# First block of a two-block transformer: a two-list scheduler replaced by one written program, PSUM pairs replaced by a ring of eight banks

## The chip, the cores and the metric

The kernel runs on one core of a Trainium2 chip. TensorE (PE) multiplies matrices and transposes; its results go to PSUM, which here is used as eight banks of 128 partitions by 512 float32 numbers. ScalarE (ACT), VectorE (DVE) and GpSimd (POOL) do the elementwise work, and only they empty PSUM banks. SyncE (SP) starts most DMA transfers. The engines run side by side, each through its own list of instructions in order, and wait for each other by semaphores. The metric is the device time of one execution in microseconds (us), the median of several.

## The reference

x is 8 x 512 x 256 in float32 (8 batches of 512 rows), with a condition per batch and 64 context tokens per batch. Block 1, per batch:

```python
mod = silu(c) @ adaln_w.T + adaln_b          # nine vectors of 256: shift, scale, gate of each part
h = modulate(ln(x), shift_sa, scale_sa)
q, k, v = ln(heads(h, 16)), ln(heads(h, 16)), heads(h, 16)   # times and plus learned rows
x = x + gate_sa * unheads(softmax(q k^T / 4) v)
h = modulate(ln(x), shift_ca, scale_ca)      # cross attention, 16 heads of 16, 64 keys
x = x + gate_ca * (unheads(softmax(q kb^T / 4) vb) @ ca_out_w.T + ca_out_b)
h = modulate(ln(x), shift_ff, scale_ff)      # feed forward, 1024 wide
x = x + gate_ff * ((silu(h @ w1.T) * (h @ w3.T)) @ w2.T)
```

Block 2 has self attention with 16 heads of 64 and rotary embeddings, cross attention, and a feed forward with gelu. Everything is float32.

## The kernel before

**Block 1's tiling.** A batch's 16 heads are handled as four groups g of four heads, and the 512 keys as four key tiles kt of 128. One unit (`block`, L593) is one group with one key tile. Its four score matmuls (L603) contract over 16 rows each and stand in four row strips of the array, so they run together as a quad; they write two PSUM tiles of two banks (`bank_s`), each emptied by one exp on ACT of 128x1024 (L606) into a p tile. Its four value matmuls (L612) make 32 columns each in four column strips, also together, and add up over the key tiles in `bank_o`; v has a column of ones, so the softmax denominator comes along. Before a group, `queries_keys` (L580) transposes the normalized heads into a bank, ACT makes q of it (L589), DVE k (L590). After a group, `group_end` (L617) copies ps_O to oT on ACT (L619), and `group_back` (L622) transposes oT into a bank; DVE takes the denominator, inverts, multiplies and checks, POOL applies the gate and adds to x.

The per-head layernorm is made a batch ahead: `norm` (L518), then for each half c of the heads `head_centre` (DVE, L558 to L560), `head_square` (ACT, L564), `head_var` (DVE) and `head_scale` (POOL: a power of 5.4 us, a product of 1.06 us).

`batch2` (L683) is the cross attention of a batch, one cycle later: `prepare` (layernorm), `turn` (eight transposes to hT), `queries`, two units `block(c)` with scores of 32 rows and values, the latter with a copy of the denominators on ACT (den, L733, one buffer), two DMAs out and one back (L736 to L738), `inverse`, `scaled`, and `project_out`. `batch3` (L769) is the feed forward, two cycles later: eight `up(f)` (four full matmuls of 512 columns, a tanh on ACT, L797, two products on DVE), and `down(t)` for four row tiles (L801).

**Order.** `run_blocks` (L51) writes the program out. A batch is a cycle of 18 units: 16 of self attention, and two of the cross attention of the batch before at places 11 and 13. Other steps are registered with `at(i, fn)` and `then(i, fn)` (L498, L501) at a unit's number. In the first cycle each unit stands alone: its scores, the values of the unit before, the other steps. Later the units go in twos: scores(i), steps registered at i-2 and i-1, scores(i+1), values(i-1), values(i), and then the steps of the list `behind`. At the start, three `awake` matmuls stand on either side of the first group's preparation to keep PE busy.

**PSUM.** S: two tiles of two banks. O: one bank. D: one. X: two. `bank_x()` (L119) takes D and X in turn for everything that is not a score or a value product of self attention. Every engine that empties a bank so decides when PE may write to it again.

**Block 2** opens its own PSUM pools (`pair`, name ps_P, and others) with `other_banks` (L993); its first matmul stands at 831.19 us in the timeline. `last_out` (L1135) takes two pairs for the last self-attention output.

Of the kernel before, what the change touches and what calls it, by code (L numbers as in the profile page):

```python
# [10 lines left out]
F32 = mybir.dt.float32  # L11
# [7 lines left out]
P = 128  # L19
# [25 lines left out]
class Block:  # L45


    def __init__(self, scores, values):
        self.scores, self.values = scores, values


def run_blocks(blocks, beside, behind, alone):

    def scores(i):
        for fn in blocks[i].scores if i < len(blocks) else []:
            fn()

    def values(i):
        for fn in blocks[i].values if 0 <= i < len(blocks) else []:
            fn()

    def others(i):
        for fn in beside.get(i, []):
            fn()

    others(-1)
    for i in range(alone):  # L70
        scores(i)
        values(i - 1)
        others(i)
    scores(alone)
    values(alone - 1)
    for i in range(alone + 1, max(len(blocks) + 2, *(k + 3 for k in (*beside, *behind))), 2):
        scores(i)
        if i > alone + 1:
            others(i - 2)
        others(i - 1)  # L80
        scores(i + 1)
        values(i - 1)
        values(i)
        for fn in (*behind.get(i - 2, []), *behind.get(i - 1, [])):
            fn()


def fast_path(ctx: ExitStack, tc: tile.TileContext, a: dict, out: bass.AP):
# [28 lines left out]

    def bank_x():
        turns[0] += 1  # L119
        n = turns[0] % (2 + len(extra))  # L120
        if n < len(extra):
            return extra[n]()
        return psum.tile([P, 512], F32, tag="X", name="ps_X", bufs=2)

    extra.append(bank_d)
# [137 lines left out]
    mod = sp.tile([P, 768], F32, name="mod")  # L263
    gb = sp.tile([P, D], F32, name="gb")
# [27 lines left out]
    def awake(n):  # L292

        ps = bank_o()
        for _ in range(n):
            mm(ps[:, 0:256], ident, chk.rearrange("p i c -> p (i c)"))
# [32 lines left out]
    mm(first_mod[:, D : 2 * D], ones, chk[0:1].rearrange("p i c -> p (i c)"), False, True)  # L329
    awake(16)  # L330
# [164 lines left out]
    blocks = []  # L495
    beside, behind = {}, {}

    def at(i, fn):  # L498
        beside.setdefault(max(i, -1), []).append(fn)

    def then(i, fn):  # L501

        (behind if 2 * CYCLE + 9 <= i < CYCLE * (B - 1) + 3 else beside).setdefault(max(i, -1), []).append(fn)

    CYCLE = H + 2
    X0, X1 = 11, 13


    def batch1(b):
        s = {}  # L510
        base = CYCLE * b

        def parts(v, c, par):

            hd = slice(8 * c, 8 * c + 8) if par is None else slice(8 * c + par, 8 * c + 8, 2)
            return v.rearrange("p t (h d) -> p t h d", d=HD0)[:, :, hd]

        def norm(n):  # L518

            if n == 0:  # L520
# [17 lines left out]
        def first_modulated(c, par=None):  # L538

            lv = parts(s["ln"], c, par)  # L540
            n = lv.shape[2]
            hv = s["hv"][:, :, 8 * c : 8 * c + 8] if par is None else s["hv"][:, :, 8 * c + par : 8 * c + 8 : 2]
            sh, sc = (parts(first_mod[:, None, i * D : (i + 1) * D], c, par).to_broadcast([P, NT, n, HD0])
                      for i in range(2))
            nc.vector.tensor_tensor(lv, lv, sc, ALU.mult)
            nc.vector.tensor_tensor(hv, lv, sh, ALU.add)

        def head_z(c, par):
# [4 lines left out]
        def head_centre(c, par=None):  # L553

            hv = s["hv"][:, :, 8 * c : 8 * c + 8] if par is None else s["hv"][:, :, 8 * c + par : 8 * c + 8 : 2]
# [4 lines left out]
            nc.vector.tensor_tensor(head_z(c, par), hv,  # L560
                                    mean[:, :, :, None].to_broadcast([*sh, HD0]), ALU.subtract)

        def head_square(c, par=None):
            nc.scalar.activation(parts(s["ln"], c, par), head_z(c, par), AF.Square)  # L564

        def head_var(c, par=None):
            sq = parts(s["ln"], c, par)
            sh = [P, NT, sq.shape[2]]
            s["var", c, par] = var = small.tile(sh, F32, tag=f"var{sh[2]}", name="var", bufs=2)
# [3 lines left out]
        def head_scale(c, par=None, eng=None):  # L573
            var, z = s["var", c, par], head_z(c, par)
# [5 lines left out]
        def queries_keys(g):  # L580

            c, par = divmod(g, 2)
            ps = bank_x()
# [3 lines left out]
            q = wk.tile([P, N], F32, tag="q", name="q", bufs=2)  # L587
            k = wk.tile([P, N], F32, tag="k", name="k", bufs=2)
            nc.scalar.activation(q, ps, AF.Identity, bias=qk_cols[:, 1:2], scale=qk_cols[:, 0:1])  # L589
            nc.vector.tensor_scalar(k, ps, col("kw"), col("kb"), ALU.mult, ALU.add)  # L590
            s[g] = (q, k)

        def block(g, kt):  # L593

            c, par = divmod(g, 2)
            pr = {}

            def score():
                q, k = s[g]
                pss = [bank_s() for _ in range(2)]  # L600
                for j in range(4):
                    r = slice(32 * j, 32 * j + HD0)
                    mm(pss[j // 2][:, j % 2, :], k[r, kt * P : (kt + 1) * P], q[r, :])  # L603
                for u in range(2):
                    pr[u] = wk.tile([P, 2, N], F32, tag="p", name="p", bufs=6)
                    nc.scalar.activation(pr[u], pss[u], AF.Exp, scale=HD0 ** -0.5)  # L606

            def value():
                if kt == 0:
                    s["o", g] = bank_o()  # L610
                for j in range(4):
                    mm(s["o", g][32 * j : 32 * j + 32, :], s["h"][:, kt, 8 * c + 2 * j + par, :], pr[j // 2][:, j % 2, :],  # L612
                       kt == 0, kt == NT - 1)

            return Block([score], [value])

        def group_end(g):  # L617
            oT = wk.tile([P, N], F32, tag="oT", name="oT", bufs=1)
            nc.scalar.copy(oT, s["o", g])  # L619
            s["oT", g] = oT  # L620

        def group_back(g):  # L622
            c, par = divmod(g, 2)
            ps = bank_x()
# [15 lines left out]
        n = 0  # L640
        for g in range(4):
            for kt in range(NT):
                while n in (X0, X1):
                    n += 1
                i = base + n
                blocks[i] = block(g, kt)
                if g == 0 and kt == 0:
                    if b == 0:
                        def before():
                            for n in range(3):  # L650
                                norm(n)
                            nc.vector.tensor_copy(qk_cols, cols[:, 0:2])
                            for fn in (first_modulated, head_centre, head_square, head_var):
                                fn(0, 0)
                            head_scale(0, 0, nc.vector)

                        at(-1, before)
                        at(0, lambda: awake(3))
                        for k, par, fns in ((0, 1, (first_modulated, head_centre)),
                                            (1, 1, (head_square, head_var, head_scale)),  # L660
                                            (3, None, (head_centre,)), (4, None, (head_square, head_var, head_scale))):
                            for fn in fns:
                                at(k, lambda fn=fn, par=par: fn(0 if par else 1, par))
                        at(5, lambda: spread(s["gate"], b, G_SA, D))
                        later.append((at, 2, lambda: first_modulated(1)))
                    else:

                        for m, k in enumerate((-11, -10, -9) if b == 1 else (-13, -12, -10)):
                            at(i + k, lambda m=m: norm(m))
                        for c in range(2):  # L670
                            for k, fn in zip(((-6, -5, -5, -5), (-3, -2, -1, -1))[c] if b == 1 else (-7, -5, -3, -3) if c else (-9, -8, -7, -7),
                                             (head_centre, head_square, head_var, head_scale)):
                                at(i + k, lambda c=c, fn=fn: fn(c))
                if kt == 0:
                    then(i - (2 if i <= CYCLE else 4), lambda g=g: queries_keys(g))
                if kt == NT - 1:
                    at(i + 1, lambda g=g: group_end(g))
                    full = 2 * CYCLE + 9 <= i < CYCLE * (B - 1)
                    then(i + ((4 if g == 2 else 1) if full else 2 + (b > 0 and n % 2 == 0)), lambda g=g: group_back(g))
                n += 1  # L680


    def batch2(b):  # L683
        s = {}
        base = CYCLE * (b + 1)

        def prepare(n):

# [12 lines left out]
        def turn():  # L701
            s["hT"] = transposed(wk2, s["z"], b, modT[:, 2:4, :], modT[:, 0:2, :])
# [1625 lines left out]
```

## Time and profile before

| what | value |
|---|---|
| median of 3 runs | 2326.92 us (2323.94 to 2333.01) |
| the profiled execution, its time | 2327.49 us |
| its span, first to last instruction | 2325.7 us |
| mean granted TensorE clock | 0.997 of full |
| exp of block 1's self attention, L606 | x256, 248.3 us, mean 1022 ns |
| score matmuls, ps_S<-q,k 16*128 | x1024, 161.3 us, mean 644 ns |
| value matmuls, ps_O<-p,h 128*32 | x1024, 131.4 us, mean 614 ns |
| cycle 0, first scores to first scores of the next batch | 18.80 to 83.50 us |
| cycle 1 | 83.50 to 145.20 us |
| cycles 3 to 6, each | 94.2 us |
| ACT, DVE, POOL busy in a cycle of 94.2 | 50.38, 43.33, 29.63 us |

Busy times are sums over instructions. Matmul records overlap one another (they are pipelined), so the mean of one is longer than the distance from one start to the next; distances are to be read from the timeline. The page's slices have 58 us each, so a cycle is about one and a half of them. The chain of waits is followed back from the last instruction; a share of PE in it means that PE's own work, and no one else's, set the end there. "idle before" in a timeline line is how long the engine had stood still before it, with the one that released it. "issue" means that no wait is visible.

### The profile page before, as it was taken

How to read it: one execution, taken by the hardware profiler on the slowest of the kernel's cores; microseconds unless marked ns; L12 is line 12 of the kernel's file. 1: busy time of each engine (PE TensorE's matmuls, PEld its weight loads, DVE VectorE, ACT ScalarE, POOL GpSimd, SP SyncE). 2: the span in 40 equal slices, each digit the busy share in tenths (PEclk: the TensorE clock that was granted, in tenths of full speed). 3: DMA queues.
4: the chain of work that ended last, by engine and by line, in shares of the span. 5: the costliest groups of instructions: out<-in, count | busy, mean ns of one | idle time of the engine just before them, and what ended most of it. 6: DMA issues, size and time to landing. Idle time of an engine off the chain costs nothing.

```text
span 2325.7 us, 30862 instructions
## 1 busy us (share of the span) xinstructions
PE 2306.7 (99%) x12372; PEld 1147.7 (49%) x12372; DVE 996.9 (43%) x1911; ACT 871.4 (37%) x1052; POOL 920.3 (40%) x581
## 2 busy tenths in 40 slices
PE   9999999999999999999999999999999999999999
PEld 4333544535445553444444443435345556567666
DVE  4554534444434534435353435353434554532110
ACT  4665555455552124333333333333422231221221
POOL 4553323232311036545454645454544554531110
PEclk9999999999999999999999999999999999999999
DMA  6120000000001100000000000000023222210000
GB/s 190 38 105 13 17 14 11 17 13 11 11 9 53 52 1 20 29 11 26 14 22 17 20 20 20 19 20 20 20 69 103 74 75 71 67 58 32 22 20 20
DMA packets 83735, 83.95 MB, mean 36 GB/s; under 512 B 42128, under 2 KB 59264, under 8 KB 83584
## 3 DMA queue, kind: packets, MB, share of 16 engines
q1 hardware_dynamic: 82104, 78.73, 11.4%
q8 instruction: 99, 1.62, 0.3%
q0 software_dynamic: 576, 2.10, 0.2%
q10 hardware_dynamic: 904, 1.07, 0.2%
q14 instruction: 52, 0.43, 0.1%
HBM read 71.83 MB, written 10.04 MB: 35 GB/s over the span
## 4 chain that ended last, share of the span: by engine, by line
PE 96%; DVE 1%; DMA 1%; issue 1%; ACT 1%; POOL 0%; SPq 0%; ACTq 0%; POOLq 0%; DVEq 0%
PE ps_P L128 40%; PE ps_X L128 21%; PE ps_S L128 13%; PE ps_D L128 10%; PE ps_O L128 9%; PE ps_X L439 1%; PE ps_X L626 1%; DMA rb<-rec 0%; PE ps_X L586 0%; ACT p L606 0%; PE ps_D L439 0%; PE ps_P L1005 0%; PE ps_D L626 0%; POOL var L577 0%; DMA rec<-rec 0%
## 5 line engine op out<-in xcount | busy, mean ns | idle before, releaser
L606 ACT ACTIVATE p<-ps_S 128x1024 f32<-128x1024 f32 x256 | 248.3, 1022 | 198.9 <-PE ps_S L128 198.2
L1066 ACT ACTIVATE p<-ps_P 128x1024 f32<-128x1024 f32 x256 | 245.0, 1026 | 95.0 <-PE ps_P L128 95.0
L128 PE MATMUL ps_P<-q,k 32*128 32x512 f32 x2048 | 238.9, 600 | 0.5 <-DVE t L1045 0.5
L1075 POOL TENSOR_TENSOR sm<-sm,p 128x1024 f32<-128x1024 f32 x64 | 175.4, 2740 | 139.2 <-ACT p L1066 139.1
L128 PE MATMUL ps_P<-p,v 128*32 128x512 f32 x2048 | 226.4, 594 | 0.0
L194 POOL TENSOR_TENSOR rstd<-rstd,mhalf 128x4 f32<-128x4 f32 x49 | 52.3, 1068 | 331.2 <-DVE rstd L193 329.9
L1034 ACT COPY v<-ps_P 128x1024 f32<-128x1024 f32 x32 | 32.4, 1013 | 376.7 <-PE ps_P L128 376.7
L128 PEld LDWEIGHTS ps_P<-q,k 32*128 32x128 f32 x2048 | 99.9, 184 | 133.3 <-issue 105.6
L128 PE MATMUL ps_S<-q,k 16*128 16x512 f32 x1024 | 161.3, 644 | 2.5 <-ACT p L606 1.5
L1075 DVE TENSOR_TENSOR sm<-sm,p 128x1024 f32<-128x1024 f32 x64 | 98.8, 1544 | 150.5 <-ACT p L1066 150.5
L577 POOL TENSOR_TENSOR var<-var,mhalf 128x32 f32<-128x32 f32 (+1 forms) x17 | 87.4, 5140 | 171.4 <-DVE var L571 168.0
L128 PE MATMUL ps_X<-hT,w 128*128 128x512 f32 x328 | 150.4, 597 | 0.0
L1073 POOL TENSOR_TENSOR sm<-p 128x1024 f32<-128x1024 f32 x32 | 79.1, 2471 | 160.3 <-ACT p L1066 160.3
L128 PEld LDWEIGHTS ps_P<-p,v 128*32 128x32 f32 x2048 | 63.3, 110 | 158.3 <-issue 134.8
L128 PE MATMUL ps_O<-p,h 128*32 128x512 f32 x1024 | 131.4, 614 | 0.8 <-ACT p L606 0.8
L1044 DVE TENSOR_TENSOR t<-ps_P,rope_c 128x1024 f32<-128x1024 f32 x64 | 78.4, 1225 | 108.0 <-POOL q L1048 65.9
L128 PE MATMUL ps_P<-hT,w_sa_wq 128*128 128x512 f32 x256 | 118.4, 605 | 0.5 <-DVE tmp L805 0.5
L1073 DVE TENSOR_TENSOR sm<-p 128x1024 f32<-128x1024 f32 x32 | 39.2, 1225 | 185.3 <-ACT p L1066 185.3
L128 PE MATMUL ps_P<-hT,w_sa_wk 128*128 128x512 f32 x256 | 115.1, 592 | 0.0
L128 PE MATMUL ps_P<-w_sa_wv,hT 128*128 128x512 f32 x256 | 114.9, 592 | 0.0
L128 PE MATMUL ps_P<-w_sa_wo,oT 128*128 128x256 f32 x512 | 112.0, 379 | 0.0
L128 PE MATMUL ps_S<-hT,w_ff_w 128*128 128x512 f32 x256 | 111.3, 592 | 0.0
(287 smaller groups left out, 3650.5 us busy)
## 6 DMA issues: line engine op xcount, KB each, us to landing
rb<-rec SPq DMA_DIRECT2D x128, 128.0 KB
rb<-rec_d SPq DMA_DIRECT2D x124, 128.0 KB
rb<-rec SPq DMA_DIRECT2D x16, 256.0 KB
out_dram<-x SPq DMA_DIRECT2D x15, 256.0 KB
x<-in_x_dram SPq DMA_DIRECT2D x7, 512.0 KB
gate<-modd SPq DMA_DIRECT2D x24, 128.0 KB
k_d<-q POOLq DMA_DIRECT2D x4, 512.0 KB, 3.2
v_d<-v SPq DMA_DIRECT2D x4, 512.0 KB
```

What stands on the lines that cost most here:

```text
L128: nc.tensor.matmul(o, lhsT, rhs, start=start, stop=stop)
L194: nc.gpsimd.tensor_tensor(r[:, :n], r[:, :n], mhalf[:, :n], ALU.pow)
L439: nc.tensor.transpose(ps[:, t * P : (t + 1) * P], z[:, t, k * P : (k + 1) * P], ident)
L577: nc.gpsimd.tensor_tensor(var, var, half, ALU.pow)
L606: nc.scalar.activation(pr[u], pss[u], AF.Exp, scale=HD0 ** -0.5)
L626: nc.tensor.transpose(ps[:, t * P : (t + 1) * P], s["oT", g][:, t * P : (t + 1) * P], ident)
L1034: nc.scalar.copy(s["v", half][:, t0 : t0 + 2, :], ps)
L1044: nc.vector.tensor_tensor(c, ps, rope_c[:, None, :].to_broadcast([P, 2, N]), ALU.mult)
L1066: nc.scalar.activation(pr, pss[u], AF.Exp, scale=HD1 ** -0.5)
L1073: eng.tensor_tensor(s["sm", g, u], s["p", g, 0, u], s["p", g, 1, u], ALU.add)
L1075: eng.tensor_tensor(s["sm", g, u], s["sm", g, u], s["p", g, kt, u], ALU.add)
```

## The change

The two lists and `run_blocks` go. The three `batch` functions become classes with one object per batch, and the order of block 1 is written out by hand in `beginning()` (batch 0), `cycle(c)` for c from 1 to 7, and `ending()`. The unit of order is a group with all four key tiles: two score quads, the list `beside` (full products), the other two score quads, the list `short` (transposes), four value quads, and a rest.

```diff
+    def bank():
+        return psum.tile([P, 512], F32, tag="bank", name="ps_B", bufs=8)
...
     def bank_x():
+        if not extra:
+            return bank()
...
+    def group(scores, beside, short, values, rest=()):
+
+        for fn in (*scores[:2], *beside, *scores[2:], *short, *values, *rest):
+            fn()
```

All of block 1 takes its PSUM from this ring of eight banks, in the order of the program: a ninth tile waits for the readers of the first. The scores of a unit take four banks, and each is emptied by an exp of its own:

```diff
-                pss = [bank_s() for _ in range(2)]
+            pss = [bank() for _ in range(4)]
...
-                    pr[u] = wk.tile([P, 2, N], F32, tag="p", name="p", bufs=6)
-                    nc.scalar.activation(pr[u], pss[u], AF.Exp, scale=HD0 ** -0.5)
+    def exponentials(pss):
+        p = [wk.tile([P, N], F32, tag="p", name="p", bufs=14) for _ in pss]
+        for i, ps in enumerate(pss):
+            nc.scalar.activation(p[i], ps, AF.Exp, scale=HD0 ** -0.5)
+        return p
...
-            q = wk.tile([P, N], F32, tag="q", name="q", bufs=2)
-            k = wk.tile([P, N], F32, tag="k", name="k", bufs=2)
+            q = wk.tile([P, N], F32, tag="q", name="q", bufs=1)
+            k = wk.tile([P, N], F32, tag="k", name="k", bufs=1)
```

The cycle, with s the batch's self attention, nxt the next one's, x the cross attention of the batch before, up and down the feed forwards of the two before that (the store and key steps are empty but in cycle 1):

```python
scores, values = of_self(s, 0)
group(scores, [keys[0], keys[1], done.out(0), done.out(1), up.prepare(0), up.prepare(1), down.down(0), up.prepare(2)],
      [s.queries_keys(1), prev.back(3), up.turn, nxt.norm(0), nxt.norm(1)], values)
scores, values = of_self(s, 1)
group(scores, [keys[2], store(0), down.down(1), x.prepare(0), x.prepare(1), up.up(0), x.prepare(2), keys[3], up.up(1)],
      [s.queries_keys(2), s.back(0), x.turn, nxt.norm(2)], values)
scores, values = of_self(s, 2)
group(scores, [keys[4], store(1), up.up(2), up.up(3), x.queries(0), x.queries(1)],
      [s.queries_keys(3), s.back(1), nxt.centre(0), nxt.square(0)], values)
group([x.score(0), x.score(1)], [keys[5], up.up(4), keys[6], up.up(5), s.back(2), nxt.var(0), nxt.scale(0), nxt.centre(1)],
      [], [x.value(0), x.value(1)])
scores, values = of_self(s, 3)
group(scores, [keys[7], store(2), up.up(6), x.inverse(0), x.inverse(1), up.up(7), x.scaled(0)],
      [nxt.queries_keys(0), nxt.square(1), x.scaled(1), nxt.var(1), nxt.scale(1)], values)
store(3)
```

(The lambdas around the steps are left out.) The copy of ps_O to oT now belongs to the last value step of a group, and so comes after `short`. In batch 0 the groups have the setup work of the later parts beside them, and `queries_keys` of groups 1 and 2 stands in the rest, after the values:

```python
group(scores, [first_modulated(fm, 0, 1), *head_of(s, 0, 1), setup, first_modulated(fm, 1)],
      [], values, [modulation_columns, s.queries_keys(1), *head_of(s, 1)])
```

Here `setup` is the copy into sc32 on DVE and the modulation products, and `head_of` centre, square, var and scale of a half.

Beside these: the modulation of batch 0 is copied from PSUM to SBUF once (`nc.scalar.copy(fm, first_mod)`) and read there; `awake` is called once with six matmuls, after the first `queries_keys`, in place of three and three; the feed forward's second product is made in two pieces of two row tiles (`project_out`) in place of four of one; the pools of the weights (kv1, ca0, ff0, wpool, nk) get `reuse_waits="tile"`; in block 2 `bank_x` rotates from another phase, and the four banks of `last_out` are taken earlier and in reversed order of pairs. The number and shapes of all matmuls stay as they were.

## The prediction

> **What bounds the kernel now.** I read the page first: the busy rows, the slices, the chain. All say TensorE.
>
> ```profile
> span 2325.7 us, 30862 instructions
> PE 2306.7 (99%) x12372; PEld 1147.7 (49%) x12372; DVE 996.9 (43%) x1911; ACT 871.4 (37%) x1052; POOL 920.3 (40%) x581
> ...
> PE 96%; DVE 1%; DMA 1%; issue 1%; ACT 1%; POOL 0%; SPq 0%; ACTq 0%; POOLq 0%; DVEq 0%
> ```
>
> PE is 99% busy and 96% of the chain, so only shorter PE time helps, and every wait of PE's is paid in full. The change touches block 1, which ends at 831.2 us, where block 2's first ps_P matmul stands in the timeline. "Busy" hides something, which the PE timeline of a steady cycle shows:
>
> ```profile
> 507.29 1.92 PE L128 MATMUL ps_O<-p,h 128*32 128x512 f32 x16
> 509.14 0.66 PE L586 MATMUL ps_X<-ident,z 128*128 128x128 f32 x4
> 509.73 1.14 PE L128 MATMUL ps_S<-q,k 16*128 16x512 f32 x8
> 510.80 1.98 PE L128 MATMUL ps_X<-hT,w 128*128 128x512 f32 x4
> 512.62 1.88 PE L128 MATMUL ps_D<-hT,w 128*128 128x512 f32 x4
> ```
>
> Columns: start, length, and the records joined in the line. A 512-column matmul leaves two records and takes 0.859 us start to start; a quad of four 16-row score tiles (R) or four 32-column value tiles (C) runs in the same 0.859. A transpose (T) takes 0.109. The score line should last 0.859 until the next starts; it lasts 1.07 (509.73 to 510.80). The transposes should last 0.44 and last 0.59. The last line follows one of its own shape. So the excess goes with a change of the array's tile shape. From all such starts of block 1, in ns: full to R 197, R to full 212, R to C 132, C to R 217, C to full 217, full or T to C 117, T to R 197, R to T 164, C to T 169; full and T share a shape (0).
>
> ACT bounds nothing overall, but ACT and DVE release PSUM banks, so I read their timelines too:
>
> ```profile
> 499.25 1.94 ACT L606 ACTIVATE p<-ps_S 128x1024 f32<-128x1024 f32 x2 [0.41 <-PE ps_S L128]
> 501.08 0.59 ACT L619 COPY oT<-ps_O 128x512 f32<-128x512 f32 x1
> 501.55 0.65 ACT L564 ACTIVATE ln<-z 128x512 f32<-128x512 f32 x1
> ```
> ```profile
> 487.08 0.81 DVE L590 TENSOR_SCALAR k<-ps_X,cols 128x512 f32<-128x512 f32 x1 [4.49 <-ACT q L589]
> 487.81 0.68 DVE L570 TENSOR_REDUCE var<-ln 128x32 f32<-128x512 f32 x1
> ```
>
> Two things to see: the copy that empties ps_O stands ahead of the next batch's square, and k waits for q, ACT's reader of the same bank.
>
> **What is removed: tile shapes.** Matmuls and transposes of block 1 are the same before and after (672 full, 658 C and 576 R matmuls, 406 T): 732.7 us. Counted in both built programs with the costs above, changes of shape fall from 337 (61.0 us) to 187 (33.9 us): -27.2 us, 8.15 to 4.17 us in a full cycle. A steady cycle now lasts 94.2 us, 86.05 of work and 8.15 of changes: nothing else is lost there. Cycles 0 to 2 lose about 25 us more, the start 4, the end 5.
>
> **What is added: waits, group by group.** I laid the new order of each engine out with the durations of the trace. An exp starts 1.235 us after its scores start (494.296 to 495.531). 128x512 exps are not in the trace; bounds are 0.46 us apart (half of the 0.92 between 1024-wide ones) and 0.53 (the largest distance between other 512-wide ACT instructions); I take 0.49, as the back-to-back copies. Two then cost 0.98 against 0.92; with 576 for 288, ACT gets 17 us more in 831, hidden where PE has other work.
>
> The dear one comes once a cycle in 1 to 6, where cross attention's scores follow group 2. From group 2's third score tile: eight exps end at 1.24 + 8 x 0.49 = 5.2; q(3) +0.78 = 5.9; k +0.81 = 6.8; back(1) on DVE (den 0.17, reciprocal 0.25, product 0.43, two checks 0.32) = 8.0; centre(0) on DVE (0.68 + 0.18 + 0.69) = 9.6; square(0) on ACT +0.64 = 10.3; oT copy of group 2, queued behind that square, +0.59 = 10.9. PE arrives earlier: scores 1.73 and a change, eight transposes, values 3.44, x.score(0) 0.86, with changes 7.8. The last bank of x.score(1) is that of ps_O in the ring, so PE waits 3.1. Queued behind the square on ACT are the copy and eight cross exps. In before the copy stands first and ps_O is not part of a ring.
>
> The other four of a cycle: group 0, 0.4 (turn waits for z from POOL; k behind late exps, as 14 p tiles hold exps 15 and 16 until the first value quad is done); group 1, 0.4; into group 3, 1.05 (den(1)'s copy on ACT needs the single den buffer, whose two DMAs land 2.28 us after the copy ends, 486.30 to 488.58; the scores' last bank waits for it); group 3 to next, 0.76 (four transposes alone cover the last exp and k). Sum 5.7 a cycle against 4.0 saved.
>
> **Clock.** Here row and rule differ.
>
> ```profile
> 85.81 2.04 PE L128 MATMUL ps_S<-q,k 16*128 16x512 f32 x8 [0.17 <-ACT p L606]
> 87.78 0.66 PE L586 MATMUL ps_X<-ident,z 128*128 128x128 f32 x4
> 88.36 1.79 PE L128 MATMUL ps_S<-q,k 16*128 16x512 f32 x8
> 90.09 3.58 PE L128 MATMUL ps_O<-p,h 128*32 128x512 f32 x16
> ...
> 80.00:100.00 20.00, 19.83 (x119) 6.44 (x118) 8.89 (x27) 12.53 (x14) 7.95 (x4) 0.91 0.30 70
> ```
>
> Score runs stretched by bank waits are followed by sixteen value records in 3.58 us, which take 1.92 elsewhere: half clock for 3.4 us, a loss of 1.7 (the last row is of the windows view, its 0.91 the granted clock). A second drop stands at 155 us. The Trainium skill, "TensorE: Matmul & The Clock Gate", Part 1, has the clock fall only after an idle window of about 3.4 us. The longest recorded gap before this drop is 0.17 us, so thin work is enough here. By the rule no 3.1 us wait costs clock; by the row each may cost 1.7. Of the 3.1, about 2.15 leave PE empty, and the scores ahead are thin too. I take six in ten: 1.1 a cycle. The rule's zero is the low bound.
>
> **Sum by stage** (us, before to after, each after being work with changes of shape, plus waits, plus clock):
> - Start: +0.75 (six awake matmuls between first q and first scores, formerly three on either side).
> - Cycle 0: 64.7 to 47.6 + 15.4 + 4 = 67.0. The copy into sc32 stands on DVE behind var(0,1), which waits for a square behind eight exps, so modulation's matmuls come 4.4 late; queries_keys stands after the values, leaving q, k exposed 1.7, 1.35 and 1.8; squares that wait for centre hold exps 0.9 and 2.75; kb 1.5; small ones 1.0. Two or three drops of 1.7: 4.
> - Cycle 1: 61.7 to 58.4 + 9 + 0.8 = 68.2: the five waits (5.7), and 3.3 because feed-forward products are not there yet; group 3 has one key product (1.72) to cover exps, with q and k as in cycle 0.
> - Cycle 2: 87.9 to 85.4 + 2 = 87.4.
> - Cycles 3 to 6: 4 x (94.2 to 86.05 + 4.17 + 5.7 + 1.1 = 97.0) = +11.2.
> - Cycle 7: -2 (no next batch, so no square ahead of the copy). Ending: 0, changes saved against new waits, +-3.
>
> Total 0.75 + 2.3 + 6.5 - 0.5 + 11.2 - 2 = +18.2.
>
> Costed at nothing: fm's copy, under the sixteen awake matmuls; q and k in one buffer, since the next transposes follow the last scores; down in two pieces, the same matmuls; weight pools with waits by tile, whose loads (DMA 10 to 23% only at 831) lie cycles ahead; block 2's bank rotation and the reversed last pairs, where ps_P's rows show 0.5 us of waits in 239. Uncovered, I bound these together at -3 to +5.
>
> The profiled execution took 2327.5 (span 2325.7 and 1.8 around it), 0.6 over the median. 2326.9 + 18.2 = 2345.
>
> **The rivals.**
> - **Waits covered.** ACT might pass the chain earlier (exps at 0.46, DVE gaps shorter) or the ring might give slack I did not see. Then the 27 saved remain, less 0 to 7: 2300 to 2307. For: ACT is 37% busy. Against: the chain is of dependent steps; eight exps at 0.46 shorten it by 0.25 of 3.1. Chance 0.18.
> - **Waits without drops**, the rule's case: +18.2 less 4.4 in cycles 3 to 6, 4.8 early, and part of cycle 2's 2, so +7 to +9: about 2335. Chance 0.23. This counts as no change: a measurement of this kernel can tell about 0.5%.
> - **Worse clock**, slower: every thin stretch drops, 1.7 more in each of seven cycles and twice that in cycles 0 and 1, +34: 2361. It decides once two stretches a cycle stay thin for a whole window. Chance 0.14.
> - **The change not doing what it says** I rule out: the built order has it as written.
> - The likeliest, as summed: 0.45, own range 2339 to 2353.
>
> The range reaches from the edge of the first rival to beyond the third: 2308 to 2366. Faster 0.19, same 0.24, slower 0.57.
>
> **What would show it.** Right: score lines x16 ahead of full ones; exp rows 128x512 near 0.60 mean; a PE wait near 3 us for ACT's oT copy once a cycle in 1 to 6; cycles of 96 to 97 from first scores to first scores; more slices under full clock in cycles 0 and 1. Wrong: steady cycles near 90, which means covered waits; or 94.2 cycles with the loss at the start. If the exps' distance is 0.55 or more, ACT is late everywhere, and all waits grow.

## The result and the profile after

The changed kernel takes 2384.42 us (median of 4, 2381.86 to 2387.7) against 2327.28 for the kernel before: ratio 1.0244, 95% interval 1.0218 to 1.0269. The forecast was 2345, with 2366 as its upper end. The sign was right, the size was not. The two profiled executions differ by 54.2 us, the medians by 57.1; what follows explains the 54.2.

The page of the changed kernel, rows as before:

```profile
span 2379.9 us, 31143 instructions
PE 2321.5 (98%) x12372; PEld 1183.2 (50%) x12372; DVE 990.6 (42%) x1879; ACT 883.8 (37%) x1341; POOL 919.5 (39%) x581
...
PEclk8889999999999999999999999999999999999999
...
PE 89%; ACT 3%; DVE 3%; DMA 2%; issue 1%; POOL 0%; SPq 0%; ACTq 0%; DVEq 0%; POOLq 0%
...
L589 ACT ACTIVATE p<-ps_B 128x512 f32<-128x512 f32 x576 | 291.7, 623 | 172.2 <-PE ps_B L88 172.1
```

Three things to see. PE's share of the chain fell from 96 to 89%: other engines now hold it. The first three slices have a granted clock under 0.9. And the narrow exps last 0.623, close to the 0.60 expected. The windows view by stage (length, then busy time of PE, PEld, DVE, ACT, POOL, then granted clock, DMA share, GB/s); the rows are of cycle 0, cycles 3 to 6, the ending, and block 2:

```profile
19.94:96.06 76.12, 63.27 (x368) 25.68 (x367) 33.15 (x101) 41.15 (x78) 30.43 (x19) 0.84 0.31 97
...
262.59:652.31 389.72, 378.30 (x2017) 189.20 (x2017) 173.81 (x440) 206.08 (x393) 118.40 (x76) 0.99 0.05 13
...
748.30:885.01 136.71, 124.59 (x443) 77.27 (x444) 52.10 (x118) 21.81 (x36) 8.56 (x8) 0.95 0.14 42
885.01:2379.90 1494.89, 1486.00 (x8155) 764.65 (x8153) 613.52 (x913) 464.02 (x549) 666.61 (x399) 1.00 0.12 35
```

Block 2, the last row, took 1494.5 before: nothing happened there. Block 1 ends at 885.0 instead of 831.2, which is 53.8 of the 54.2. I split each stage into PE's work (start to start distances, as in the prediction), changes of tile shape at the costs read before, and the rest, which is waiting and lost clock:

| stage | before | after | shape changes, before and after | rest, before and after | forecast of the difference | measured |
|---|---|---|---|---|---|---|
| start | 17.3 | 18.5 | 0.5, 0.5 | 3.8, 3.0 | +0.75 | +1.1 |
| cycle 0 | 64.7 | 76.1 | 7.7, 4.0 | 11.3, 26.9 | +2.3 | +11.4 |
| cycle 1 | 65.5 | 74.4 | 6.5, 4.2 | 5.6, 16.0 | +6.5 | +8.9 |
| cycle 2 | 86.3 | 92.2 | 6.9, 4.2 | 7.6, 15.7 | -0.5 | +5.9 |
| cycles 3 to 6 | 376.8 | 389.7 | 31.3, 16.7 | 1.5, 28.9 | +11.2 | +12.9 |
| cycle 7 and ending | 219.1 | 232.7 | 8.6, 4.8 | 6.6, 26.6 | -2 | +13.6 |
| sum | | | 61.5, 34.3 | 36.4, 117 | +18.2 | +53.8 |

The stages of the kernel before are cut where 128 score records a batch have passed, in both kernels alike: batch 2's first scores stand at 148.97 us, batch 3's at 235.25, batch 7's at 612.07. The cuts given ahead of the prediction (145.20, and 233.1 and 609.9 behind it) are up to 3.8 us early, since what starts at 145.2 is the last score unit of batch 1. The forecast column is as recorded. Reckoned from the early cuts, it has some 2 us too much in cycles 1 to 6.

The start's longer stage is work: three more of the awake matmuls stand ahead of the first scores. Shape changes fell by 27.2 us, as counted. The rest rose by 81. Of it, stretches in which matmuls stand at twice their distance (half clock) cost 31.2 us after and 5.6 before, as read from the distances. The granted clock itself stood at half for 78.5 us of block 1 after and 10.2 before; the matmuls that ran in that time would have needed about 35 and 5 us less at full clock.

The steady cycle, as forecast: PE, then ACT, then DVE.

```profile
318.79 2.03 PE L88 MATMUL ps_B<-q,k 16*128 16x512 f32 x16
...
321.78 3.64 PE L88 MATMUL ps_B<-p,h 128*32 128x512 f32 x32
325.35 2.26 PE L88 MATMUL ps_B<-q,kb 32*128 32x512 f32 x14
329.77 1.12 PE L88 MATMUL ps_B<-q,kb 32*128 32x512 f32 x2 [2.17 <-ACT oT L565]
```
```profile
328.62 0.63 ACT L518 ACTIVATE ln<-z 128x512 f32<-128x512 f32 x1 [3.99 <-DVE z L514]
329.15 0.57 ACT L565 COPY oT<-ps_B 128x512 f32<-128x512 f32 x1
```
```profile
325.39 0.17 DVE L579 COPY den<-ps_B 128x16 f32<-128x16 f32 x1
...
327.36 1.16 DVE L514 TENSOR_TENSOR z<-h,mean 128x512 f32<-128x512 f32 x1
```

Score and value lines are now x16 and x32. The square (L518) stood 3.99 us at the head of ACT waiting for centre's z; the copy behind it could have started at 325.4, where the values end, and PE's last cross score waited for that copy. The wait ends 10.98 us after group 2's third score tile began; 10.9 had been worked out for the copy.

The waits view of PE in block 1 after:

```profile
PE ps_B L88 <- ACT oT L565: 13.0, 6, 2.2
PE ps_B L88 <- DVE k L544: 9.3, 9, 2.2
PE ps_B L401 <- DVE z L187: 7.1, 3, 3.1
PE ps_B L88 <- DVE oT L660: 6.4, 4, 4.3
PE ps_B L88 <- DVE sc L741: 4.4, 1, 4.4
```

These are full stops (how long, how often, the longest). In the kernel before, the first line of this view is:

```profile
PE ps_X L128 <- DVE oT L752: 1.8, 1, 1.8
```

And the ending, which I had put at nothing:

```profile
814.37 4.15 PE L88 MATMUL ps_B<-w,hid 128*128 128x256 f32 x18 [2.47 <-DVE hid L697]
...
823.76 4.97 PE L88 MATMUL ps_B<-w_o,oT 128*128 128x256 f32 x14 [4.26 <-DVE oT L660]
...
838.77 4.00 PE L401 MATMUL ps_B<-ident,z 128*128 128x128 f32 x16 [3.12 <-DVE z L187]
```

### The profile page after: what moved, and what is told of

It is laid out like the page before. It is cut to its first block, busy times and chain, and to the rows that moved or that the text cites. A ratio compares the mean times of both kernels' runs of the same rounds, so it can differ in the third digit from the quotient of the medians.

```text
span 2379.9 us, 31143 instructions
## 1 busy us (share of the span) xinstructions
PE 2321.5 (98%) x12372; PEld 1183.2 (50%) x12372; DVE 990.6 (42%) x1879; ACT 883.8 (37%) x1341; POOL 919.5 (39%) x581
## 3 DMA queue, kind: packets, MB, share of 16 engines
q1 hardware_dynamic: 82104, 78.73, 11.3%
q8 instruction: 100, 1.64, 0.3%
## 4 chain that ended last, share of the span: by engine, by line
PE 89%; ACT 3%; DVE 3%; DMA 2%; issue 1%; POOL 0%; SPq 0%; ACTq 0%; DVEq 0%; POOLq 0%
PE ps_P L88 40%; PE ps_B L88 26%; PE ps_X L88 7%; PE ps_S L88 6%; PE ps_D L88 5%; PE ps_O L88 4%; ACT p L589 2%; DMA rb<-rec 1%; DVE k L544 1%; PE ps_B L401 1%; ACT q L543 1%; DMA den<-den 0%; PE ps_B L572 0%; PE ps_B L540 0%; DVE z L514 0%
## 5 line engine op out<-in xcount | busy, mean ns | idle before, releaser
L589 ACT ACTIVATE p<-ps_B 128x512 f32<-128x512 f32 x576 | 291.7, 623 | 172.2 <-PE ps_B L88 172.1
L88 PE MATMUL ps_B<-hT,w 128*128 128x512 f32 x512 | 235.1, 614 | 0.0
L88 PEld LDWEIGHTS ps_B<-hT,w 128*128 128x128 f32 x512 | 98.4, 196 | 131.3 <-issue 106.1
L88 PE MATMUL ps_B<-q,k 16*128 16x512 f32 x1024 | 144.6, 629 | 11.1 <-DVE k L544 9.3
L583 POOL TENSOR_TENSOR attn<-attn,gate 128x256 f32<-128x256 f32 x32 | 23.3, 728 | 303.1 <-DVE attn L581 302.0
L88 PE MATMUL ps_B<-p,h 128*32 128x512 f32 x1024 | 120.4, 604 | 0.0
L88 PE MATMUL ps_B<-w,hid 128*128 128x256 f32 x512 | 115.4, 384 | 2.5 <-DVE hid L697 2.5
```

What stands on the lines that cost most here:

```text
L88: nc.tensor.matmul(o, lhsT, rhs, start=start, stop=stop)
L589: nc.scalar.activation(p[i], ps, AF.Exp, scale=HD0 ** -0.5)
```

## The experiments

My theory after the result: the saving in shape changes is real, and what outweighs it are instructions that stand at the head of ACT's or DVE's queue waiting for another engine, with PE behind them, plus the half clock after such stretches. Rivals: the narrow exps themselves; the ring of eight as such; a clock that falls for another reason. Each run is compared with the kernel before on its own chip; edits are against the changed kernel, but for e5. Differences between two experiments are between medians. The kernel before had medians from 2326.7 to 2329.3 on these chips, so a difference of 3 us between runs on two chips says little.

**e1: square after the values.**

```diff
-              [s.queries_keys(3), s.back(1), nxt.centre(0), nxt.square(0)], values)
+              [s.queries_keys(3), s.back(1)], values, [nxt.centre(0), nxt.square(0)])
```

> The changed kernel, with centre(0) and square(0) of the next batch issued after the values of group 2 instead of before them, so that the copy of the value bank stands first on ScalarE. Theory (queue order on ScalarE makes the wait, the wait makes the clock fall): the stretch of 3.55 us at the second cross score pair goes in all six cycles (-21), and with it the four half-clock stretches that follow it in cycles 1, 2, 4 and 5 (1.7 to 3.4 each, -8.5): about 2355. Rival, the wait is the ring's own (cross scores need eight fresh banks, whoever empties them): an exp becomes the releaser, -5 at most: about 2380. Rival, the clock is not tied to these waits: -21 alone: about 2363.

Measured 2375.83, ratio 1.0204 (1.0187 to 1.0221): a quarter of what was expected. From the timeline of all engines:

```profile
327.09 0.59 ACT L565 COPY oT<-ps_B 128x512 f32<-128x512 f32 x1 [0.94 <-PE ps_B L88]
...
330.15 0.63 ACT L518 ACTIVATE ln<-z 128x512 f32<-128x512 f32 x1 [2.47 <-DVE z L514]
...
330.69 4.00 ACT L589 ACTIVATE p<-ps_B 128x512 f32<-128x512 f32 x8
...
331.32 4.07 PE L88 MATMUL ps_B<-hT,w 128*128 128x512 f32 x5 [2.25 <-ACT p L589]
```

The copy is early now, but the square still stands ahead of the cross exps and still waits for DVE; PE stops one product later, for an exp. My edit was half of one: the stretch shrank from 3.55 to 2.52. The first rival described what happened, but for another reason, which e6 settles.

**e6: square behind the cross exps.**

```diff
-              [s.queries_keys(3), s.back(1), nxt.centre(0), nxt.square(0)], values)
+              [s.queries_keys(3), s.back(1)], values, [nxt.centre(0)])
...
-              [keys[5], up.up(4), keys[6], up.up(5), s.back(2), nxt.var(0), ...
+              [keys[5], up.up(4), keys[6], nxt.square(0), up.up(5), s.back(2), nxt.var(0), ...
```

> The changed kernel, with centre(0) after the values of group 2 and square(0) after the cross exps and one up product's tanh, so that nothing on ScalarE between the last value and the cross exps waits for VectorE. Theory, as amended by the first run (any instruction of ScalarE that waits for VectorE there holds PE, through the copy or through the exps): the stretch at the cross scores goes in six cycles (3.3 each, -20), and the half-clock stretches behind it (-8): about 2357. Rival (the ring itself is the wait, whoever is late): another releaser takes its place and most of the 3.3 stays, above 2372.

Measured 2355.50, ratio 1.0122 (1.0098 to 1.0147): 29 us less, by the place of one 0.63 us instruction and what stands behind it. PE at the cross scores:

```profile
315.45 2.19 PE L88 MATMUL ps_B<-q,kb 32*128 32x512 f32 x16
317.58 7.13 PE L88 MATMUL ps_B<-hT,w 128*128 128x512 f32 x16
```

Sixteen records without a stop. The ring didn't hold PE; the waiting instruction did. Half-clock loss went from 31.2 to 21.1 us with it (time at half from 78.5 to 54.6).

**e2: batch 0 in another order.** The copy into sc32 first, centre of the later half ahead of the squares, and q and k in the middle of the values:

```diff
-        group(scores, [first_modulated(fm, 0, 1), *head_of(s, 0, 1), setup, first_modulated(fm, 1)],
-              [], values, [modulation_columns, s.queries_keys(1), *head_of(s, 1)])
+        group(scores, [tensor_copy(sc32[:, :, 0:B], scT), first_modulated(fm, 0, 1), half[0],
+                       modulation, half[1], first_modulated(fm, 1), whole[0], *half[2:]],
+              [], values[:2], [modulation_columns, s.queries_keys(1), *values[2:], *whole[1:]])
```

(Groups 1 and 3 likewise; in group 2, centre moves ahead of back(1).)

> The changed kernel, with batch 0 in another order: the copy into sc32 first on VectorE, centre of the later half ahead of the squares, and the transposes for the next group's q and k between the second and third value quads instead of behind the fourth. Theory: the waits for sc (4.4) and for k (1.8, 2.3, 1.8) and for the square (2.5) go or shrink to a third, and of the six half-clock stretches of cycle 0 some four: cycle 0 from 76.1 to about 62, the whole about 2370. Rival, the first cycle is bound by ScalarE's 64 narrower exps whatever the order: cycle 0 stays above 72, the whole above 2380.

Measured 2370.65, ratio 1.0184 (1.0167 to 1.0201). Cycle 0 went from 76.1 to 61.6, under the 64.7 of before. So it was order, and 64 narrow exps fit into it.

**e3: the ending in another order.** Inverses after the last up product, the last piece of each prepare ahead of the down product, block 2's loads after both scaled steps:

```diff
-        for fn in (up.up(6), x.inverse(0), x.inverse(1), open_block1, up.up(7), x.scaled(0), ..., up.down(0), x.scaled(1),
-                   x.out(0), x.out(1), ..., up.down(1), last.prepare(2), first_norm(2), first_turn, last.turn):
+        for fn in (up.up(6), up.up(7), x.inverse(0), x.inverse(1), x.scaled(0), up.down(0), x.scaled(1), open_block1, ...,
+                   x.out(0), x.out(1), ..., last.prepare(2), up.down(1), first_norm(2), first_turn, last.turn):
```

> The changed kernel, with another order in the ending: both inverses after the last up product, block 2's weight loads after both scaled steps, and the last piece of each prepare (which writes z) ahead of the down product whose result VectorE waits for. Theory: VectorE's order makes four waits (2.0, 2.5, 4.3, 3.3) and the clock stretches behind them: the ending from 136.7 to about 124, the whole about 2372. Rival, the weight loads alone make the denominators' transfers late: only the 4.3 goes, about 2379. Rival, DMA latency as such: no change.

Measured 2380.34, ratio 1.0215 (1.0198 to 1.0232): 4 us less, a third of it. The wait for hid went, that for z fell to 1.84, but a transfer took their place:

```profile
811.62 0.62 SPq L656 DMA_DIRECT2D rb<-rec  x1
...
812.34 0.41 SPq L654 DMA_DIRECT2D rec<-rec  x1
...
812.80 0.42 SPq L136 DMA_DIRECT2D w_sa_wo<-in_sa_wo_dram  x1
...
818.28 0.69 DVE L660 TENSOR_TENSOR oT<-oT,rb 128x512 f32<-128x512 f32 x1 [6.38 <-DMA rb<-rec]
...
819.12 1.19 PE L88 MATMUL ps_B<-w_o,oT 128*128 128x256 f32 x2 [5.51 <-DVE oT L660]
```

The weights are loaded between the denominators' transfers although the program has them later: in the built program these loads stand ahead of what the text has before them. The place in the text is not the place in SP's queue. The kernel before has such loads among its small transfers too (SP's timeline from 748.86 to 760.40), and its rb took 4.4 and 7.2 us from issue to use; PE lost only the 1.8 us shown above, having other work.

**e7: e3, with the loads held.** A memset of one column of each weight tile, on DVE behind both scaled steps:

```diff
+        if name in ("sa_wq4", "sa_wk4", "sa_wv", "sa_wo"):
+            nc.vector.memset(w[:, 0:1], 0.0)
```

> The changed kernel with the ending in the other order, and with block 2's four weight loads (4 MB) held back until VectorE has done both scaled steps: a one-column memset of each weight tile stands there. Theory, as amended by the third run (the order frees two waits, and the loads fill the DMA engines while the small transfers of the denominators are on their way): waits for rb from 5.5 and 3.7 to under 2 together, waits for z to under 3; ending from 136.7 to about 123, the whole about 2371. Rival (the chain of four small transfers is late by itself, because both halves of the cross attention now end together): rb waits stay above 5 us, the whole above 2376.

Measured 2373.03, ratio 1.0199 (1.0174 to 1.0223): 11 us less than the changed kernel, near the 13 expected. The first rb now takes 3.7 us from issue to use, 6.7 in e3, so the loads did hold it up. The waits for rb didn't fall under 2 together, though: 1.7, and 3.8 more that the view names by the memset which stands directly behind the second scaled step. That is 5.5 where e3 has 9.2, so on the waits the rival's mark (above 5) was met. With a single rb buffer the second transfer starts after the first has been used, so that part is the chain's own. The ending is 6.1 us shorter than e3's. PE's full stops there fell by 2.5 us; most of the other 3.6 is clock: the granted clock stands at half for 3.4 us of it, in e3 for 17.1, in the changed kernel for 13.7.

**e4: matmuls of no use in the waits.**

```diff
+            for _ in range(fill):
+                mm(pss[0][:, 0:256], ident, chk.rearrange("p i c -> p (i c)"))
```

> The changed kernel, with matmuls of no use put into the waits, into banks that the next product overwrites: 18 ahead of the first modulation products, 7 or 9 ahead of the first scores of groups 1 and 2 and of batch 1, 10 ahead of the second cross scores of each cycle (103 in all, 22 us at 0.216 each if nothing covered them). Theory (empty stretches halve the clock, and that is a third or more of the loss): waits stay as long as they are, half-clock stretches in cycles 1 to 6 behind the cross scores (8.5) and half of those of cycle 0 (5) go: about 2371, mean clock up from 0.983 to 0.99. Rival, the clock falls for another reason: clock unchanged, time 2384 to 2406.

Measured 2398.84, ratio 1.03 (1.0283 to 1.0318): slower by 14, where 13 less was expected. I had mis-costed the filler: a 256-column matmul is two records of 0.216, so 0.43, and 103 of them are 44 us, not 22.

```profile
328.44 1.14 PE L88 MATMUL ps_B<-q,kb 32*128 32x512 f32 x8
329.66 4.58 PE L88 MATMUL ps_B<-chk,ident 128*128 128x256 f32 x20
334.18 1.14 PE L88 MATMUL ps_B<-q,kb 32*128 32x512 f32 x8
```

The filler is longer than the wait it fills (5.74 us from the first cross scores to the last, 4.42 in the changed kernel). As a test of time it failed; of the clock it says what was asked: mean clock 0.988 for 0.983, half-clock loss 23.5 us for 31.2 (time at half 54.6 us for 78.5), and no half-clock stretch behind the cross scores in cycles 1 to 6, where the changed kernel has them in four. Filled, the stretch keeps its clock.

**e5: the kernel before with narrow exps.**

```diff
-                    nc.scalar.activation(pr[u], pss[u], AF.Exp, scale=HD0 ** -0.5)
+                    for i in range(2):
+                        nc.scalar.activation(pr[u][:, i, :], pss[u][:, i, :], AF.Exp, scale=HD0 ** -0.5)
```

> The kernel before, with each exp of 128x1024 in block 1 cut into two of 128x512; nothing else changes. Theory (the narrow exps are not the loss; their 17 us of ScalarE time lie beside other work): 0 to +5, nearly all of it in cycles 0 to 2, where score runs already wait for exps: 2327 to 2332. Rival (narrow exps make ScalarE late everywhere, and that is what the changed kernel pays): +15 or more.

Measured 2332.13, ratio 1.0018 (1.0008 to 1.0029), 4 us more. That rival is out as the cause of 57.

**e9: all mends** (e2, e6 and e7, and the turns of cycles 1 and 2 after the values).

> The changed kernel with all mends at once: square behind the cross exps, batch 0's order, the ending's order with held loads, and the turns of cycles 1 and 2 after the values. Theory (waits and the half clock after them add up and are the whole loss): 2384 - 27 - 14 - 13 - 5 = about 2325, at the kernel before or a little under, clock above 0.99. Rival (mending one wait uncovers the next, since each bank of the ring follows the one before): less than two thirds of the sum, above 2345.

Measured 2326.18, ratio 0.9995 (0.9982 to 1.0008). 58 us less than the changed kernel. The three parts that were measured alone give 29, 14 and 11, so 54; the turns were not run alone, and 5 was expected of them. The rival, that each mend uncovers the next wait, is out for these four. In its trace shape changes cost 35.1 and the rest 61.2.

**e10: e9 with the products beside a group split in two**, which adds shape changes and nothing else:

```diff
+    def halved(at, scores, beside, *more):
+
+        group([scores[0], *beside[:at], scores[1]], [], [], [], [*beside[at:]])
+        group(scores[2:], [], *more)
```

> The kernel with all mends, with the products beside a group split in two: one score quad, half of them, the second quad, the other half, in the four self-attention groups of cycles 1 to 7. Same work; each split adds one change from row tiles to full and back, 0.41 us by the costs read in the kernel before, about 26 times. Theory (changes of shape are paid in full, so the change's saving of 27 us is real): +11, about 2337. Rival (ScalarE's lead counts for more: exps come spread out, so waits shrink by as much): within 3 us of 2326, or below.

Measured 2331.99, ratio 1.0015 (1.0003 to 1.0028): 5.8 more than e9, half of the forecast and twice the rival's. The trace has 48 more changes than e9's, 9.8 us at the costs read before. The profiled executions differ by 13 us, all of it up by the end of cycle 2, and 9.7 of it in cycle 0, which the edit leaves alone: PE has the same order there in both, and the granted clock stands at half for 27.3 us instead of 6.8. So the whole time proves nothing on the price of a change. The later cycles that have full clock in both traces do better: 92.9 us in e9, 93.3 in e10. Eight more changes add 1.64 at the costs read before, and the rest falls by 1.16, since the products between the quads give the exps time and the stretch of 1.15 at group 3 is gone; the two together give the 0.5 measured. Theory and rival were both half right.

**e12: e9 with two den buffers and 13 p tiles. e11: the same, with two more mends (not shown).**

```diff
-            den = wk2.tile([P, N], F32, tag="den", name="den", bufs=1)
+            den = wk2.tile([P, N], F32, tag="den", name="den", bufs=2)
...
-        p = [wk.tile([P, N], F32, tag="p", name="p", bufs=14) for _ in pss]
+        p = [wk.tile([P, N], F32, tag="p", name="p", bufs=13) for _ in pss]
```

> All mends, and two den buffers with 13 p tiles, without the other two additions. Theory: -11, about 2315, and no stretch over 0.3 us at group 3's scores. Rival (p tiles): the last value quad of each group waits longer than the 0.65 us of now, and the whole is 2322 or more.

> All mends, and in addition: two buffers for den (paid for with 13 p tiles instead of 14), var and scale of the first batch's odd heads ahead of the other half's modulation on VectorE, and the weight tiles' memsets after the last cross projection. Theory (what is left are waits of this kind): the 1.15 us at group 3's scores in seven cycles go (-8), with half of the clock stretches behind them (-3), 2.9 at the first transposes of batch 0, 3 in the ending: about 2309, under the kernel before by 0.6 to 0.9%. Rival (13 p tiles cost more than den gives): 2320 or more.

Measured 2327.62 (0.9995, 0.9984 to 1.0007) and 2325.87 (0.9984, 0.9976 to 0.9993): both rivals. The stretch at group 3 is gone, but PE now stops for k behind the values three times a cycle instead of once (0.5 us each, 15 times in cycles 3 to 7 of e12 and 5 times in e9). One p tile fewer gives back what the second den saves: cycles at full clock last 93.2 us in e12, 92.9 in e9. What e11's two other mends do can't be told from 1.8 us.

**e13: e11 with 14 p tiles**; the room comes from elsewhere, and the ending's order changes once more (not shown):

```diff
-                s["gate"] = gate = wk2.tile([P, D], F32, tag="gate", name="gate", bufs=3)
+                s["gate"] = gate = wk2.tile([P, D], F32, tag="gate", name="gate", bufs=2)
...
-            gb = wk2.tile([P, D], F32, tag="gb", name="gb", bufs=1)
+            gb = wk2.tile([P, 2, D], F32, tag="tmp", name="tmp", bufs=1)[:, 0, :]
```

> All mends with the two later additions, two den buffers with all 14 p tiles (the room comes from two gate buffers in place of three, and from cross attention's bias row in the scratch tile of the output step), and a down product ahead of the last but one cross output in the ending. Theory (the second den saves the 1.15 us a cycle and clock behind it, and the thirteenth-tile ring had given it back as 0.65 us in each group and 0.56 at the cross scores, about 3 us a cycle): 2326 less 8, 3, 2 and 2, about 2311, under the kernel before by 0.5 to 0.9%. Rival (what is left moves on to the next late instruction, as it did with 13 tiles): 2322 or more.

Measured 2310.39 (2308.56 to 2315.14), ratio 0.9929 (0.9915 to 0.9942), the one version that beats the kernel before by more than half a per cent. PE's longest waits in block 1:

```profile
PE ps_B L88 <- DVE oT L662: 6.2, 3, 3.7
PE ps_B L403 <- DVE z L189: 3.0, 2, 2.7
```

Cycles 3 to 6 last 91.7 us each, 2.5 under the kernel before, at full clock in both: the work is the same 86.0, changes of shape cost 3.7 less, and the rest is 1.2 more. Here the saving shows as time. The longest wait left is the ending's for rb; the ending didn't gain from the new order (130.7 us, 129.3 in e9).

## Why the prediction was wrong

The steady cycle came out nearly as laid out; what failed is the sum by stage around it. The waits at both ends were put too low, the ending at nothing, and of half clock about 11 us were put in where 31.2 came. Of the 35.6 us by which block 1 missed the forecast, the clock term makes about 20.

**Right.** "changes of shape fall from 337 (61.0 us) to 187 (33.9 us): -27.2 us": 61.5 to 34.3 in the traces, by the same costs; e13's steady cycles show the saving as time. The waits of a steady cycle: 5.7 forecast, 6.0 measured where the clock held (3.55 at the cross scores, 1.15 at group 3, 0.65 at the end, small ones for the rest); of the first, 2.17 as a full stop, 2.15 forecast. (The terms given for PE's arrival there add up to 7.4 and not 7.8; with 7.4 the forecast 3.1 would have been the 3.5 measured.) Cycles 3 to 6: +12.9 for +11.2. The wait for sc: 4.4 and 4.36. "Costed at nothing" for block 2, fm, q and k in one buffer, down in two pieces, waits by tile: block 2 differs by 0.4; the others were not varied alone, but all of them are in e9 and e13, which are back at the kernel before or under it.

**Right by luck.** "I take six in ten" for the clock behind the cross scores: four of six. No reason was given for six, and the last part shows that it hung on where a fixed grid of time fell.

**Wrong, in order of size.**
- "Ending: 0, changes saved against new waits, +-3", with cycle 7 at -2: +13.6 measured. This step failed by 15.6. I had laid out the steady cycle's queues and not the ending's, where DVE stands waiting for a transfer (hid late by 2.5), for PE (z late by 1.8 and 3.1, queued behind the gate product of a down step), and where both halves of the cross attention end together, just as 4 MB of weights are loaded. e3 and e7 show each part; behind these stretches the granted clock stood at half for 13.7 us, some 6 us of PE's time.
- Cycle 0, "47.6 + 15.4 + 4 = 67.0", measured 76.1: work with its changes was 49.3, so 1.7 of it was left out of the sum, and the rest 26.9 instead of 19.4. The waits were the ones named; half clock took 8.5 where 4 was put. e2 shows that order made them.
- Cycle 1, "58.4 + 9 + 0.8 = 68.2", measured 74.4: the work was exact (58.3), the rest 16.0, half clock 5.3 of it. Cycle 2, "85.4 + 2 = 87.4", which is work of 76.4 and a rest of 11, measured 92.2: the rest was 15.7, half clock 5.2 of it, and up.turn waits 2.2 for z with no down product to cover it.
- Taken across stages, the clock term is the mis-sized one: I put 0.8 and nothing of note in cycles 1 and 7 and the ending, and counted thin stretches as cross-score waits alone. Measured half-clock loss is 31.2 us; the forecast has about 11 (4, 0.8, 2 and 4.4). The third rival, "worse clock", named this mechanism and reckoned +34 for the whole; it left the ending out as the likeliest case did, and so the range did not reach.

## What to carry to other kernels

An order written by hand must be followed on every engine's queue, at both ends of the program as closely as in the middle: ask of every instruction of ACT and DVE what it waits for, and who stands behind it. Here one square of 0.63 us at the wrong place cost 29 us, about a third of it by the half clock behind the wait. When shape changes or other overheads are taken out of a PE that was 99% busy, the cover that they gave to other engines goes too (put back in e10, 1.64 us of changes a cycle took 1.16 us of waits away); and where buffers are short, count all rings together, since one p tile was worth as much as a second den.

## What the runs showed of the hardware

- The clock halves behind stretches that are thin, not empty. In the changed kernel it did so behind 2.17 us of full stop, in four of six equal cases, and the same 3.55 us stretch kept full clock in cycles 3 and 6. Only two full stops of block 1 are longer than 3.4 us (4.36 and 4.26), while the clock fell 16 times.
- What makes the difference between equal cases is a grid of time. In all 14 traces every change of the granted clock lies on multiples of 3.413 us, counted from a first mark that stands between 4.4 and 7.2 us in the different executions. Two pairs of neighbouring grid stretches, from cycle 3 and cycle 5 (length, busy times, then granted clock):

```profile
325.68:329.09 3.41, 1.93 (x14) 0.65 (x6) 2.67 (x7) 0.47 (x1) 1.45 (x2) 1.00 0.00 0
329.09:332.51 3.42, 2.74 (x6) 1.16 (x7) 0.00 (x0) 3.42 (x9) 0.00 (x0) 1.00 0.00 0
...
520.24:523.65 3.41, 1.43 (x10) 0.46 (x4) 2.28 (x6) 0.96 (x2) 1.45 (x2) 1.00 0.00 0
523.65:527.07 3.42, 3.23 (x4) 1.21 (x5) 0.00 (x0) 3.42 (x9) 0.00 (x0) 0.50 0.00 0
```

For each grid stretch, take the share of the array that matmuls fill, over time: rows times columns out of 128 x 128, for the distance that the matmul takes, so that a quad of 16-row scores counts half and a stop nothing. In block 1 of the 14 traces the clock fell 128 times, always behind a grid stretch with a share of 0.38 or less; of the 3163 grid stretches behind which it stayed full, 17 had that little. At the cross scores of cycles 1 to 6 the thinnest grid stretch has 0.16, 0.20, 0.35, 0.35, 0.23 and 0.35; it fell in cycles 1, 2, 4 and 5, and in 3 and 6 the grid had cut the stop in two. So thin score runs count almost like stops, and the same program can draw a better or a worse grid: e12's ending, in text the same as e9's, took 132.7 us with 10.2 at half, e9's 129.3 with 3.4. This is a count over the traces; no run was made to test it, and 0.35 goes both ways.
- The order of DMA issues on SP's queue is not that of the program's text: loads went ahead between small transfers, and one of those, rb, then took until 818.28 from 811.62 (e3); without loads beside it, 3.7 us (e7).
- A 128x512 exp lasts 0.623 us, eight in a row 4.03, so 0.49 apart, the distance taken from copies.
